# The second block's gathers and diagonals issued earlier, subtractions and casts moved between engines, in a ternary feed-forward kernel

## The chip, the cores and the metric

One core of a Trainium2 chip runs the whole kernel. The metric is the time of one execution on the device in microseconds (us). The kernel before was run three times: median 1070.45 us, from 1069.66 to 1070.65. One further execution was recorded by the hardware profiler; it took 1070.15 us, and its recorded span is 1068.3 us.

The engines are named as in the profile: PE is TensorE (matrix multiplication), PEld its weight loads, DVE is VectorE, ACT is ScalarE, POOL is GpSimd, SP is SyncE, which issues most transfers. Each engine runs its own instructions in order and waits on semaphores for the others.

## The reference

Cut to what matters, the reference computes:

```python
u  = einsum('bct,bcd->bdt', x, weights[conditions])   # x: 128 x 64 x 512, weights: 200 x 64 x 64
W1q = ternarize(W1); W2q = ternarize(W2)              # W1: 2048 x 512, W2: 512 x 2048
h  = gelu(einsum('bsd,hd->bsh', u, W1q) + b1)         # exact GELU
y  = einsum('bsh,dh->bsd', h, W2q) + b2
out = x + fake_quant_4bit(y)                          # one scale for the whole of y

def ternarize(W):
    delta = 0.05 * max|W|;  mask = |W| > delta
    alpha = sum(|W| where mask) / max(sum(mask), 1)
    return alpha * sign(W) * mask
```

Every one of the 128 samples has its own 64 x 64 matrix, chosen by `conditions`. The 128 x 64 = 8192 rows ("tokens") then pass through two ternary layers. A layer's alpha is known only when its whole weight matrix has been compared with the threshold, and the threshold only when the whole matrix has been read.

## The kernel before, in words

**Tiling.** The samples are taken in pairs, four pairs (512 tokens) to a block, 16 blocks (`NB`). In a block each pair is multiplied by a 128 x 128 block-diagonal matrix that holds two samples' matrices (`mix`, in four matmuls of 128 columns). The hidden dimension is taken in 16 chunks of 128 (`NH`). For a chunk, layer 1 (`layer1`) is eight matmuls of 512 columns: four slices of the input times two, because each activation is split into a rounded high part and the remaining low part (`split`: a copy by ScalarE, a subtraction by VectorE) so that the multiplication keeps full precision. `bend` applies GELU with alpha as its scale on ScalarE and splits the result in the same way. Layer 2 (`layer2`) is eight matmuls of 512 columns for each chunk, accumulated over the 16 chunks in four PSUM tiles `py`.

**Weights.** Signs and masks of the weights are kept as ternary values `terns` (W1) and `terns2` (W2), in four groups of four chunks. Before a chunk is multiplied, `widen1` or `widen2` casts its ternary weights to the 32-bit type of the matmul into one of four small buffers (`w1f`, `w2f`), mostly on GpSimd. From the second block on the weights are kept in 8 bits (`w1t`, `w2t`), made by `kept` on ScalarE.

**The start.** The change concerns only block 0 and the making of block 1's inputs. While W1 arrives, 54 matmuls into an unused tile (`idle`, L286 to L289) keep TensorE busy. GpSimd issues four gathers, one for each pair (`fetch`, L185: a row of `weights` for every partition, through an indirect transfer that GpSimd issues itself), into four buffers `wg`, and copies them onto the block diagonal of `diag` (`place`, L197: two copies of 64 x 64). VectorE takes the maximum of |W1|; a copy and a transpose on TensorE spread it over the partitions (`spread`, L229), in program order behind the idle matmuls; then come the threshold, block 0's mixes (`mix0`) and their splits (`hi0`, `lo0`), the masks (`mask1`), the products with the signs (`signed1`) and the first weight casts.

**Alpha of W1.** `count1` counts a group's mask by eight matmuls with a matrix of ones into `number`; `above1` sums max(|W| - delta, 0) on ScalarE. `alpha_1` (L492) reduces both: the count first, then, after its `yield`, the sums through a small matmul `total`. No GELU can run before alpha, so `early` runs layer 1 ahead into five PSUM slots, and `early_bend` follows. Chunk 5 needs the slot of chunk 0, and so its GELU. In program order the matmuls are: chunks 0 and 1, count of group 0, chunk 2, count 1, chunk 3, counts 2 and 3, total, chunk 4.

**The rest of block 0.** A loop over hc = 5 to 15 runs chunk hc of layer 1, the cast for chunk hc + 2 and `early_bend(hc - 4)`. `behind` places W2's work between: maxima (`largest2`), threshold (in `ahead` for hc = 11), and `signed2(g)`, the ternary values of W2's group g: a compare into half `g % 2` of the tile `junk` and a combined compare and subtract, both on VectorE. The low part of the split of chunks 0, 2, 4, 6, 8, 10 and 12 is a subtraction on GpSimd, at once; that of the others is put off (`open_low`) and issued on VectorE by `low`. The casts of chunks 7, 9, 11, 13 and 15 are on ScalarE. A second loop over hc = 0 to 13 (L645) runs layer 2 of block 0, the cast for chunk hc + 2, `kept`, the counts `count2(g)` on ScalarE (into half `g % 2` of `junk` again), the sums `sum2` on VectorE, and for block 1 a gather in each of hc = 0 to 3, a `place` in each of hc = 4 to 7, and a mix with its split (`condition`) in hc = 6, 8, 10 and 12. The order of instructions on each engine is the program's order (`InOrder`, L47). Layer 1 of block 1 follows; from block 2 to 12 a seven-product scheme with fewer matmuls (`seven`) takes its place, and at the end the scale of the quantization is found and all of x is read again to write the output.

Of the kernel before, what the change touches and what calls it, by code (L numbers as in the profile page):

```python
# [58 lines left out]
def tile_cond_ternary_ffn(  # L59
# [12 lines left out]
    pe, act, dve, pool, sp = (  # L72
        InOrder(tc, e) for e in (nc.tensor, nc.scalar, nc.vector, nc.gpsimd, nc.sync)
    )
    B, C, T = x.shape
    S, _, D = weights.shape
    NT = T // P
    NH = W1.shape[1]
    assert 2 * C == P and 2 * D == P and C == D and W1.shape == (P, NH, NT, P)
    PAIRS = 4  # L80
    BLK = PAIRS * P
    NB = B // (2 * PAIRS)
    NG = 4
# [51 lines left out]
    for g in range(NG):  # L135
        w = big.tile([P, GH, T], F32, tag="big", name=f"nat1_{g}")
# [6 lines left out]
    for g in range(NG):  # L143
        w = big.tile([P, GH, T], F32, tag="big", name=f"nat2_{g}")
# [30 lines left out]
    def half_of(h):  # L175
        return slice(h * C, (h + 1) * C)
# [8 lines left out]
    def fetch(n, j):  # L185

        pair = n * PAIRS + j
        wg = gather.tile([P, D], F32, tag="wg", name=f"wg_{pair}")
        pool.indirect_dma_start(
            out=wg[:, :],  # L190
            out_offset=None,
            in_=table,
            in_offset=bass.IndirectOffsetOnAxis(ap=rows[:, pair : pair + 1], axis=0),
        )
        return wg

    def place(j, wg):  # L197
        for h in range(2):
            pool.tensor_copy(diag[half_of(h), j, h * D : (h + 1) * D], wg[half_of(h), :])
# [36 lines left out]
    def thresholds(w, top, room):  # L236

        top1 = const.tile([P, 1], F32, name=f"top1_{w}")
        dve.tensor_reduce(top1, top, AX.X, ALU.max)
        delta = const.tile([P, 1], F32, name=f"delta_{w}")  # L240
        tops = spread(top1, delta, room)
        yield
        dve.tensor_reduce(delta, tops, AX.X, ALU.max)
        dve.tensor_scalar(delta, delta, THRESHOLD, None, ALU.mult)
        minus = const.tile([P, 1], F32, name=f"minus_{w}")
        dve.tensor_scalar(minus, delta, -1.0, None, ALU.mult)
        yield delta, minus
# [9 lines left out]
    def flat(w):  # L257
        return w.rearrange("p a b -> p (a b)")
# [4 lines left out]
    terns = [big.tile([P, 2, WCH], BF16, tag="big", name=f"terns_{i}") for i in range(2)]  # L263
# [5 lines left out]
    def group1(tiles, g):  # L269
        return tiles[g // 2][:, g % 2, :]  # L270

    def sign1(g):
        act.activation(group1(signs, g), flat(nat1[g]), AF.Sign)
# [11 lines left out]

    idle = ps_h.tile([P, T], F32, tag="ph", name="idle")  # L286
    pool.memset(above[:, :T], 1.0)
    for _ in range(54):
        pe.matmul(out=idle, lhsT=ones_b, rhs=above[:, :T], start=True, stop=True)  # L289
    at = 0  # L290
    for g in range(NG):
# [12 lines left out]
    fetched = [fetch(0, j) for j in range(PAIRS)]  # L304
# [13 lines left out]
    def lo0(j):  # L318
        part = slice(j * P, (j + 1) * P)
        dve.tensor_tensor(  # L320
            two_next[1][:, :, part], pcs[j], two_next[0][:, :, part], ALU.subtract
        )

    find = thresholds("w1", top_1, first[:, 3, :P])
# [7 lines left out]
    def mask1(g, part=slice(0, WCH)):  # L332

        dve.tensor_scalar(
            group1(masks, g)[:, part], flat(mags[g])[:, part], delta1, None, ALU.is_gt
        )

    def signed1(g, part=slice(0, WCH)):
        dve.tensor_tensor(
            group1(terns, g)[:, part],  # L340
            group1(masks, g)[:, part],
            group1(signs, g)[:, part],
            ALU.mult,
        )

    def count1(g, number, first, final):
        n = number.shape[1]
        for i in range(WCH // n):
            pe.matmul(
                out=number,  # L350
                lhsT=ones_b,
                rhs=group1(masks, g)[:, i * n : (i + 1) * n],
                start=(first and i == 0),
                stop=(final and i == WCH // n - 1),
            )
# [22 lines left out]
    def widen1(n, hc):  # L378

        if n == 0:  # L380
            w = w1f[hc % 4]
            g, i = divmod(hc, GH)
            src = group1(terns, g)[:, i * T : (i + 1) * T]
            if hc > 6 and hc % 2 == 1:
                act.copy(flat(w), src)
            else:
                pool.tensor_copy(flat(w), src)
        else:
            w = w1f[hc % 2]
            pool.tensor_copy(flat(w), w1t[:, hc])  # L390
        wide1[n, hc] = w
# [16 lines left out]
    def layer1(n, hc, ph, pieces=1, between=None):  # L408

        w = wide1.pop((n, hc))  # L410
        for i in range(pieces):
            part = slice(i * BLK // pieces, (i + 1) * BLK // pieces)
            for c in range(NT):
                if between is not None and c == NT // 2:
                    between()
                for k in range(2):
                    pe.matmul(
                        out=ph[:, part],
                        lhsT=w[:, c, :],
                        rhs=cond[n][k][:, c, part],  # L420
                        start=(c == 0 and k == 0),
                        stop=(c == NT - 1 and k == 1),
                    )

    def bend(n, hc, ph, two, hf, engine=dve):
        act.activation(hf, ph, AF.Gelu, bias=b1t[:, hc : hc + 1], scale=alpha[1])
        if engine is None:
            act.copy(two[0], hf)
            open_low[n, hc] = lambda: dve.tensor_tensor(two[1], hf, two[0], ALU.subtract)
        else:  # L430
            split(hf, *two, engine)
        hidden[n, hc] = two
# [3 lines left out]
    def low(n, hc):  # L436

        open_low.pop((n, hc), lambda: None)()
# [36 lines left out]
    def early(hc, between=None):  # L475

        slot = (hc + 1) % 5
        if slot < 2:
            ph = ps_h.tile([P, BLK], F32, tag="ph", name=f"ph_0_{hc}")
        else:  # L480
            ph = ps_y.tile([P, BLK], F32, tag=f"py{slot - 2}", name=f"ph_0_{hc}")
        layer1(0, hc, ph, 2 if hc == 0 else 1, between)
        waiting[hc] = ph

    def early_bend(hc):
        if hc % 2 == 0:
            pairs0[hc // 2] = big.tile([P, 2, 2, BLK], F32R, tag="big", name=f"h_{hc}")
        two = [pairs0[hc // 2][:, hc % 2, k, :] for k in range(2)]
        on_pool = hc % 2 == 0 and hc < NH - 2
        bend(0, hc, waiting.pop(hc), two, ring[hc % len(ring)], pool if on_pool else None)  # L490

    def alpha_1():  # L492
# [67 lines left out]

    mask1(0, parts1[0])
    signed1(0, parts1[0])
    widen1(0, 0)
    widen1(0, 1)
    lo0(0)
    lo0(1)
    hi0(2)
# [12 lines left out]
    number = ps_y.tile([P, T // 2], F32, tag="py3", name="number")  # L580
    count1(0, number, True, False)
    mask1(1)
    signed1(1)
    widen1(0, 4)
    mask1(2)
    mask1(3)
    early(2)
    count1(1, number, False, False)
    early(3)
    count1(2, number, False, False)  # L590
    count1(3, number, False, True)
    find = alpha_1()
    next(find)
    signed1(2)
    next(find, None)
    widen1(0, 5)
    early(4)
    early_bend(0)
# [3 lines left out]
    find = thresholds("w2", top_2, above.bitcast(F32)[:, :P])  # L602
# [6 lines left out]
    def behind(hc):  # L609
        if 5 <= hc < 5 + NG:  # L610
            largest2(hc - 5)
        if hc == 6:
            sign1(3)
        if hc == 9:
            signed1(3)
        if hc == 11:
            delta.extend(next(find))
            signed2(0)
        if hc == 12:
            low(0, 1)  # L620
            low(0, 3)
            signed2(1)
        if hc in (13, 14):
            widen2(0, hc - 13)
# [7 lines left out]
        behind(hc)  # L632
    for hc in range(NH - 4, NH):
        early_bend(hc)
    for hc in (5, 7, 9, 11):
        low(0, hc)

    w1t = big.tile([P, NH, T], F8, tag="big", name="w1t")
# [6 lines left out]
    for hc in range(NH - LAG):  # L645
        if hc + 2 < NH - LAG:
            widen2(0, hc + 2)
        layer2(0, hc)
        if hc < PAIRS:
            fetched.append(fetch(1, hc))  # L650
        elif hc < 2 * PAIRS:
            place(hc - PAIRS, fetched[hc])
        if hc == 0:
            signed2(2)
        if hc == 1:
            for i in (13, 14, 15):
                low(0, i)
        if hc < NG:
            kept(w1t, hc, terns)
        if hc == 3:  # L660
            signed2(3)
        if hc == 4:
            two_next = parts(1)
            w2t = big.tile([P, NH, T], F8, tag="big", name="w2t")
        if 4 <= hc < 4 + 2 * NG:
            g = (hc - 4) // 2
            if hc % 2 == 0:
                count2(g)
            else:
                kept(w2t, g, terns2)  # L670
        if hc in (6, 8, 10, 12):
            j = (hc - 6) // 2
            condition(1, j, pair_of(x_next, j), two_next)
            sum2(j)
    cond[1] = two_next
    x_next, two_next, fetched = [], [], []
# [282 lines left out]
    while s < len(steps):  # L959
        n, hc = steps[s]  # L960
# [116 lines left out]
```

## Time and profile before

| what | value |
|---|---|
| median of three runs | 1070.45 us (1069.66 to 1070.65) |
| profiled execution | 1070.15 us |
| its span | 1068.3 us, 16722 instructions |
| PE busy (matmul) | 990.0 us, 93% |
| DVE busy | 610.8 us, 57% |
| ACT busy | 614.4 us, 58% |
| POOL busy | 629.5 us, 59% |
| granted TensorE clock, 0 to 1000 us | 1.00 |

The parts of the profile that are used below: a table of busy times by stretch (the stretch, its length, then busy time and number of instructions of PE, PEld, DVE, ACT and POOL, then the granted clock, the DMA share and GB/s); the chain of waits, which follows the work that ended last back to the start (start, duration, what; "xN" is a number of instructions in one piece); and the timeline of one engine (start, duration, engine, line, operation, output <- inputs, shapes; in brackets the idle time before it and what ended that). Line L55 stands for nearly everything, since a helper on that line issues the instructions; so instructions are told apart by their tiles. The names are those of the program: `wg` a gather, `diag` a diagonal, `wf` a widened weight, `ph` layer 1's result, `py` layer 2's, `pc` a mix, `ring` a GELU's output, `h` its split parts, `x` the split inputs.

### The profile page before, as it was taken

To read this page: it belongs to the slowest core of one execution; us is meant where nothing else is said; L and a number is where in the kernel's file an instruction comes from. 1 tells how busy PE (TensorE), PEld (TensorE's weight loads), DVE (VectorE), ACT (ScalarE), POOL (GpSimd) and SP (SyncE) were. 2 spreads that over 40 slices of the span, in tenths; PEclk is the share of its full clock that TensorE was granted. 3 is DMA by queue.
4 is the path that set the end of the run, shared out by engine and by line. 5 is a ranking of instruction groups with operands and counts; after the bars stand their busy time and mean duration, and the time that the engine had idled before them with its cause. 6 is when DMAs were issued, how large, how long until landed. Compare 5 with 4: busy or idle time off the path is not lost.

```text
span 1068.3 us, 16722 instructions
## 1 busy us (share of the span) xinstructions
PE 990.0 (93%) x5764; PEld 864.0 (81%) x5765; DVE 610.8 (57%) x1075; ACT 614.4 (58%) x1045; POOL 629.5 (59%) x1014
## 2 busy tenths in 40 slices
PE   8989999999999999999999999999999999999400
PEld 5768889999999999999999999999998888888300
DVE  7786736565656556565656656565655223231692
ACT  7885445666666666656666665666655334334481
POOL 4595747676666667576666667576664435333242
PEclk9999999999999999999999999999999999999855
DMA  9100000100000010100000010001001010041899
GB/s 363 47 25 1 14 31 6 30 15 22 23 19 26 15 32 5 31 14 24 23 22 24 13 33 4 30 17 30 16 21 42 3 40 6 1 148 30 294 412 374
DMA packets 26611, 62.19 MB, mean 58 GB/s; under 512 B 3488, under 2 KB 3488, under 8 KB 25760
## 3 DMA queue, kind: packets, MB, share of 16 engines
q1 hardware_dynamic: 19872, 42.25, 11.7%
q0 software_dynamic: 6656, 18.88, 4.6%
q8 instruction: 46, 0.75, 0.3%
q14 instruction: 37, 0.30, 0.1%
HBM read 44.34 MB, written 16.78 MB: 57 GB/s over the span
## 4 chain that ended last, share of the span: by engine, by line
PE 91%; DMA 3%; DVE 2%; ACT 2%; POOL 1%; issue 1%; SPq 1%; POOLq 0%; DVEq 0%; ACTq 0%
PE py L55 43%; PE xy L55 16%; PE ph L55 13%; PE z L55 12%; PE pc L55 5%; DMA xt<-in_x 3%; PE idle L55 1%; DVE y L55 1%; ACT diag L55 1%; SPq L55 1%; POOL wg L55 0%; POOL diag L55 0%; ACT ring L55 0%; PE number L55 0%; DVE ymax L55 0%
## 5 line engine op out<-in xcount | busy, mean ns | idle before, releaser
L55 PE MATMUL py<-wf,h 128*128 128x512 f32 x2048 | 532.6, 395 | 4.4 <-POOL wf L55 3.5
L55 PEld LDWEIGHTS py<-wf,h 128*128 128x128 f32 x2048 | 364.9, 189 | 70.4 <-POOL wf L55 5.5
L55 DVE TENSOR_TENSOR h<-ring,h 128x512 fp32r<-128x512 f32 x249 | 193.8, 780 | 182.6 <-ACT h L55 182.6
L55 POOL CAST wf<-w2t 128x512 fp32r<-128x512 fp8e4 x242 | 173.0, 715 | 151.3 <-PE py L55 147.7
L55 ACT ACTIVATE ring<-ring,b1t,alpha_w 128x512 f32<-128x512 f32 x176 | 144.3, 820 | 97.9 <-DVE ring L55 97.9
L55 POOL CAST wf<-w1s 128x256 fp32r<-128x256 fp8e4 (+1 forms) x264 | 133.9, 512 | 110.0 <-PE xy L55 80.6
L55 POOL CAST wf<-w1t 128x256 fp32r<-128x256 fp8e4 (+1 forms) x240 | 156.9, 659 | 56.9 <-PE ph L55 45.6
L55 ACT CAST h<-ring 128x512 fp32r<-128x512 f32 x256 | 158.9, 621 | 8.2
L55 PE MATMUL ph<-x,wf 128*128 128x512 f32 (+1 forms) x648 | 158.2, 388 | 2.4 <-ACT ring L55 1.7
L55 ACT ACTIVATE ring<-ph,b1t,alpha_w 128x512 f32<-128x512 f32 x80 | 62.3, 779 | 141.9 <-PE ph L55 141.8
L55 PEld LDWEIGHTS ph<-x,wf 128*128 128x128 f32 x648 | 119.8, 188 | 28.7 <-issue 2.4
L55 DVE TENSOR_TENSOR ring<-xy,ring 128x256 f32<-128x256 f32 (+1 forms) x176 | 97.2, 552 | 64.3 <-PE xy L55 64.3
L55 PEld LDWEIGHTS xy<-xt,wf 128*128 128x128 f32 x704 | 107.6, 189 | 14.1
L55 PE MATMUL xy<-xb,wf 128*128 128x256 f32 x704 | 112.4, 281 | 0.0
L55 PE MATMUL xy<-xt,wf 128*128 128x256 f32 x704 | 111.8, 282 | 0.0
L55 PEld LDWEIGHTS xy<-xb,wf 128*128 128x128 f32 x704 | 102.2, 190 | 7.9
L55 ACT COPY ring<-xy 128x256 f32<-128x256 f32 x176 | 65.1, 370 | 67.8 <-PE xy L55 67.7
L55 PE MATMUL z<-xt,wf 128*128 128x256 f32 x704 | 98.3, 282 | 0.0
L55 ACT COPY ring<-z 128x512 f32<-128x512 f32 x88 | 51.7, 588 | 73.9 <-DVE h L55 73.3
L55 PEld LDWEIGHTS z<-xt,wf 128*128 128x128 f32 x704 | 90.2, 190 | 0.0
L55 DVE TENSOR_TENSOR xt<-x_quarters,xt 128x512 fp32r<-128x512 f32 x44 | 33.8, 768 | 90.9 <-ACT xt L55 90.9
L55 POOL DMA_INDIRECT wg<-in_L_cond_weights,rows x64 | 76.3, 1193 | 11.4 <-issue 5.4
(104 smaller groups left out, 857.7 us busy)
## 6 DMA issues: line engine op xcount, KB each, us to landing
xt<-in_x SPq DMA_DIRECT2D x36, 512.0 KB, 6.6
out<-y POOLq DMA_DIRECT2D x30, 512.0 KB, 12.5
x_quarters<-in_x SPq DMA_DIRECT2D x48, 256.0 KB, 2.6
nat<-in_L_ffn_W SPq DMA_DIRECT2D x6, 1024.0 KB, 10.1
nat<-in_L_ffn_W SPq DMA_DIRECT2D x3, 512.0 KB, 9.0
wg<-in_L_cond_weights,rows POOLq DMA_INDIRECT x64, 2.7
w1t<-in_x SPq DMA_DIRECT2D x4, 256.0 KB, 2.7
w2t<-in_x SPq DMA_DIRECT2D x4, 256.0 KB, 2.6
```

Of the source, the lines that this page charges most:

```text
L55: return lambda *args, **kw: self._tc.keep_in_program_order(make(*args, **kw))
```

## The change

Six edits, all ahead of the second block's layer 1:

- 50 idle matmuls in place of 54.
- The casts of chunks 7, 9, 11, 13 and 15 of W1 go from ScalarE to GpSimd.
- GpSimd keeps the subtractions of chunks 0, 2, 4 and 6; those of 8, 10 and 12 are put off and done by VectorE (`low`), in a new grouping: 5, 7, 8, 9 behind layer 1, and 10 to 15 in the second turn of layer 2's loop.
- Block 1's gathers move out of layer 2's loop: three ahead of the first two weight casts on GpSimd, the fourth behind them. Its diagonals are placed behind the cast of chunk 4, ahead of that of chunk 5.
- Layer 1 of chunk 3 comes behind all counts; `signed1(2)` ahead of the count's reduction; the total of alpha's sums is issued within chunk 3, ahead of its last slice.
- `sign1(3)` moves one chunk back, and block 1's mixes one turn forward, to hc = 5, 7, 9 and 11.

```diff
-    for _ in range(54):
+    for _ in range(50):
         pe.matmul(out=idle, lhsT=ones_b, rhs=above[:, :T], start=True, stop=True)
...
-            src = group1(terns, g)[:, i * T : (i + 1) * T]
-            if hc > 6 and hc % 2 == 1:
-                act.copy(flat(w), src)
-            else:
-                pool.tensor_copy(flat(w), src)
+            pool.tensor_copy(flat(w), group1(terns, g)[:, i * T : (i + 1) * T])
...
-                if between is not None and c == NT // 2:
+                if between is not None and c == NT - 1:
                     between()
...
-        on_pool = hc % 2 == 0 and hc < NH - 2
+        on_pool = hc in (0, 2, 4, 6)
...
     signed1(0, parts1[0])
+    fetched += [fetch(1, j) for j in range(3)]
     widen1(0, 0)
     widen1(0, 1)
+    fetched += [fetch(1, 3)]
     lo0(0)
...
     widen1(0, 4)
+    for j in range(PAIRS):
+        place(j, fetched[PAIRS + j])
     mask1(2)
     mask1(3)
+    signed1(2)
     early(2)
-    count1(1, number, False, False)
-    early(3)
-    count1(2, number, False, False)
-    count1(3, number, False, True)
+    for g in range(1, NG):
+        count1(g, number, False, g == NG - 1)
     find = alpha_1()
     next(find)
-    signed1(2)
-    next(find, None)
+    early(3, lambda: next(find, None))
     widen1(0, 5)
     early(4)
     early_bend(0)
...
-        if hc == 6:
+        if hc == 7:
             sign1(3)
...
-    for hc in (5, 7, 9, 11):
+    for hc in (5, 7, 8, 9):
         low(0, hc)
...
-        if hc < PAIRS:
-            fetched.append(fetch(1, hc))
-        elif hc < 2 * PAIRS:
-            place(hc - PAIRS, fetched[hc])
...
         if hc == 1:
-            for i in (13, 14, 15):
+            for i in range(10, NH):
                 low(0, i)
...
-        if hc in (6, 8, 10, 12):
-            j = (hc - 6) // 2
+        if hc in (5, 7, 9, 11):
+            j = (hc - 5) // 2
             condition(1, j, pair_of(x_next, j), two_next)
```

More of the change, by code (lines that the diff above doesn't have):

```diff
@@ L619, in behind @@
         if hc == 12:
-            low(0, 1)
-            low(0, 3)
+            for i in (1, 3):
+                low(0, i)
             signed2(1)
```

## The prediction

> **What bounds the kernel now.** I read the page first (one core, span 1068.3 us, the profiled execution 1070.15 us, so 1.85 us lie around the span; the median of the runs shown is 0.30 us above that execution). Then the busy time by stages:
>
> ```profile
> 20.00:40.00 20.00, 17.98 (x106) 14.24 (x105) 16.55 (x19) 16.21 (x19) 9.79 (x10) 1.00 0.36 146
> 40.00:60.00 20.00, 19.63 (x88) 15.83 (x87) 17.14 (x14) 19.62 (x30) 14.21 (x11) 1.00 0.19 54
> 60.00:80.00 20.00, 15.02 (x65) 10.76 (x64) 17.32 (x14) 15.20 (x13) 18.90 (x21) 1.00 0.10 34
> 80.00:100.00 20.00, 20.00 (x103) 17.02 (x102) 11.40 (x12) 12.49 (x14) 11.98 (x12) 1.00 0.00 0
> 180.00:1000.00 820.00, 819.13 (x4919) 729.42 (x4918) 441.40 (x876) 462.66 (x862) 493.04 (x835) 1.00 0.09 27
> ```
>
> After the stretch come TensorE (matmuls, then loads), VectorE, ScalarE, GpSimd. From 80 us to 1000 us TensorE is full, so the change, which lies wholly ahead of that, is worth exactly what it takes from the start of the second block's layer 1. In the chain of waits that start is the "PE ph" piece at 93.28:
>
> ```profile
> 16.23 1.03 PE idle L55 x4
> 17.26 0.11 PE tops_delta_w L55
> 34.96 0.79 ACT ring L55
> 57.66 3.64 PE py L55 x16
> 67.56 2.83 POOL wg L55
> 71.18 0.64 POOL wg L55
> 74.28 2.35 POOL diag L55
> 91.45 1.83 PE py L55 x8
> 93.28 1.81 PE ph L55 x8
> ```
>
> Three places lose time: the warm-up still runs when the threshold could be spread (VectorE's copy ends at 15.84 + 0.23 = 16.07); alpha (34.87) holds the first GELU and so layer 1 of chunk 5 (35.88); and from 61 to 77 us layer 2's weight casts queue on GpSimd behind subtractions, gathers and diagonals. The last takes 93.28 - 57.66 = 35.62 us for 14 layer-2 chunks (1.82 each, 25.5) and four mixes (0.89 each, 3.56): 6.6 us lost.
>
> The timeline of ScalarE shows a second limit:
>
> ```profile
> 60.68 7.30 ACT L55 CAST w1t<-terns 128x2048 fp8e4<-128x2048 bf16 x4
> 69.58 1.91 ACT L55 ACTIVATE junk<-terns 128x2048 bf16<-128x2048 bf16 x1 [1.60 <-DVE terns L55]
> 76.55 1.91 ACT L55 ACTIVATE junk<-terns 128x2048 bf16<-128x2048 bf16 x1 [3.17 <-DVE terns L55]
> ```
>
> The count of group 1 overwrites the junk half that signed2(3) uses, so it waits for signed2(3)'s end at 76.51. Behind it on ScalarE stand the casts that split the second block's inputs.
>
> [...] four GpSimd casts at 23.74 took 1.6 us apiece, ending in step with VectorE's masks and products, where alone they take 0.59. [...] gathers took 0.94 us early and 1.23 to 2.83 here. [...] here idle matmuls reach 0.213 us from 8.03 on, so four fewer at the end leave the clock warm.
>
> **The change part by part.**
>
> *Four fewer idle matmuls.* 41 took 8.73 us, so 4 x 0.213 = 0.85. The spread could then start at 16.25, after 16.07: -0.85 on the threshold, mixes and masks.
>
> *Gathers early.* Three gathers go ahead of the first weight casts on GpSimd, which idles from 15.93 to 19.60. The early row gives 1.48 + 1.28 + 1.26 us with gaps, to 19.95; the mask and product run meanwhile (17.1 to 18.6), so I take 20.2. First cast to 20.8 (before 20.19), so layer 1 starts at about 20.9 and its second half at about 21.8, against 22.34: 0.5 of the 0.85 survives. Bounds: [...] each gather at the 2.83 row plus 0.17 gap ends at 24.9, which makes that start 4.8 later than 20.70. The fourth gather (1.3 to 2 us) fits before widen1(0,2), whose input is ready at about 22.8. Their transfers (6.2 us to landing under the weight load) are back by 29 us, in time for the diagonals. SP's queue is not passed.
>
> *Diagonals early.* Eight copies of 0.23 us stand between widen1(0,4) and widen1(0,5). VectorE then runs two masks and signed1(2); one small copy slips between two of these, so three are done by 30 and five more by 31.6, then widen1(0,5) by 32.2. It is needed at 34. On VectorE I charge 0.3 us more for these interruptions (bounds 0 and 1.5, the excess of 0.35 per cast seen on the masks times four).
>
> *Counts ahead of chunk 3, alpha within it.* Masks end near 29.0, the last count near 30, signed1(2) is now ahead of the count's reduction (1.21) and hidden, since ScalarE's sums end at 31.74 - 0.85 = 30.9 anyway. TensorE meanwhile does three quarters of chunk 3 (1.4), then the total (0.12). Alpha is at about 32, not 34.87. TensorE has the rest of chunk 3 and chunk 4 to about 34.1; the GELU ends at 32.9. So chunk 5 starts at 34.1, not 35.88: -1.8 (bounds -2.3 and 0).
>
> *ScalarE's five casts to GpSimd, GpSimd's three subtractions to VectorE.* ScalarE loses 5 x 0.62 = 3.1 us, so one chunk takes 1.33 there against 1.82 on TensorE; even with sign1(3) (1.81) behind chunk 3, chunk 9 has 1 us to spare. GpSimd gains 5 x 0.61 and loses subtractions of 3.29, 1.74 and 3.31. Layer 1 then runs 11 x 1.822 + 0.11 = 20.15 without the former stalls (1.6): it ends at 54.25, not 57.66. Moving sign1(3) one chunk back costs nothing: signed1(3) waits for VectorE's four reductions (8.86) longer. Layer 2 and mixes, 29.06 us, would end at 83.3.
>
> *VectorE's chain to signed2(3).* It starts when the second threshold's transpose runs ahead of chunk 11: 34.1 + 6 x 1.82 + 0.3 + 0.7 = 46.1, say 46.2 (before 49.29). It holds 4 x (1.28 + 2.35) = 14.5 and now twelve subtractions, not nine: 12 x 0.69 = 8.3; 22.8 in all. Before, the same minimum was 20.7 and the measured length 27.2[...]. I estimate about 14 casts there now, some 8 us of work, giving 4.5 (4.1 by ratio, 4.9 at 0.35 each). So 27.3, and signed2(3) ends at 73.5, not 76.51.
>
> *ScalarE after it.* Count 1.91 + kept 1.80 + split cast 0.56, then rounds of 4.18 (80.72 to 84.90): the last split cast ends 12.7 after signed2(3), VectorE's low part 13.4 after. Layer 1 of the second block starts at 73.5 + 13.45 = 86.95. TensorE stands some 3.6 us here: this is the new wait, "PE ph from DVE x".
>
> **Sum.** 93.28 - 86.95 = 6.3 us gained. The profiled 1070.15 becomes 1063.85 (span 1062.0), the median 1070.45 becomes **1064.1**. Nothing behind the point changes order, and the tail (39 us of transfers) starts that much earlier.
>
> **Rivals.**
>
> *TensorE alone bounds (12 in 100).* [...] its chain has the minimum: 45.7 + 22.8 = 68.5, plus 13.45 = 82. TensorE then sets 82.8 and the gain is 10.5: 1060.0. For: GpSimd is relieved of all gathers. Against: its casts are there, and each one contends.
>
> *The early gathers hold the first cast (13 in 100 for it and lesser delays).* At 3.0 us each layer 1 starts at 25.5; 12.9 us of work follow, chunk 5 starts at 38.4, the second chain at about 50.5, signed2(3) at 77.8, the second block at 91.2: 1068.4, the edge of no change. Milder forms end between 1066.5 and 1068. [...]
>
> *Same (8 in 100).* Two half-measures of this kind together, within 0.2%: 1068.3 to 1072.6, which is about what a measurement can tell from no change.
>
> *Slower (7 in 100).* [...] At the worst means and longest seen (2.32 + 2.86 per group, 1.40 per subtraction) its chain is 4 x 5.18 + 12 x 1.40 = 37.5; signed2(3) ends at 83.7 and the second block starts at 97.1, 3.9 later: 1074.3. It turns slower where signed2(3) passes 79.8, a chain over 33.6. For: VectorE is the busiest feeder in that stretch. Against: GpSimd's long subtractions, its worst partner, leave it.
>
> The likeliest (60 in 100) lies between gains of 4 and 9: 1061.5 to 1066.5. The range for 8 in 10 is 1060.2 to 1068.0. Faster 0.85, same 0.08, slower 0.07.
>
> **What would show it.** The spread at 16.25; gathers on GpSimd from 15.95 and the first cast ending near 20.8; GELU 0 near 32, chunk 5 at 34.1 with no wait on the ring; layer 2 starting near 54.3 and no wait on casts in it; signed2(3) ending near 73.5, ScalarE's second count waiting for it; a TensorE idle of about 3.6 us ahead of the second block's layer 1 at 87. Wrong, if that idle is absent (then faster), or if the first cast or signed2(3) comes as late as before.

## The result, and the profile after

The changed kernel takes 1063.66 us in the median (1062.84 to 1064.56), the kernel before, run beside it, 1070.5. The ratio is 0.9938, 95% interval 0.9921 to 0.9955: faster by 0.45% to 0.79%. The forecast was 1064.1. The profiled execution took 1062.89 us, its span is 1061.0 us.

The busy times of the changed kernel by the same stretches (columns as before: TensorE, its loads, VectorE, ScalarE, GpSimd, then the granted clock):

```profile
20.00:40.00 20.00, 19.43 (x111) 16.06 (x110) 18.69 (x18) 18.42 (x20) 16.50 (x22) 1.00 0.39 154
40.00:60.00 20.00, 20.00 (x90) 16.51 (x89) 17.84 (x18) 19.46 (x27) 18.09 (x14) 1.00 0.27 80
60.00:80.00 20.00, 20.00 (x106) 17.15 (x105) 18.20 (x16) 14.62 (x13) 9.66 (x9) 1.00 0.00 1
80.00:100.00 20.00, 17.73 (x74) 13.17 (x74) 13.39 (x21) 9.55 (x13) 9.68 (x12) 1.00 0.01 2
```

TensorE is now full from 40 to 80 us, where it was at 19.63 and 15.02 of 20; but from 80 to 100, where it was full, 2.3 us are missing. So the wait moved. The chain of waits says to where. Pieces of it, in order:

```profile
15.76 0.25 POOL diag L55
18.97 0.95 POOL wg L55
20.63 4.01 PE ph L55 x24
31.54 13.39 PE ph L55 x58
44.92 0.12 PE tops_delta_w L55
63.41 4.85 DVE h L55 x6
69.85 2.61 DVE terns L55
72.49 2.00 ACT junk L55 x2
84.63 0.50 ACT x L55
85.15 0.70 DVE x L55
85.89 1.89 PE ph L55 x7
```

Before, between 20 us and the second block, this chain ran mainly on TensorE, ScalarE and GpSimd's gathers and diagonals. Now it leaves TensorE at the transpose of W2's threshold (44.92), runs through VectorE to the end of signed2(3) at 72.46, through ScalarE's counts, `kept` casts and split casts to 85.13, and comes back at 85.89, where "PE ph" is layer 1 of the second block. That is 7.39 us earlier than the 93.28 of before, and the spans differ by 7.3.

The wait itself, in ScalarE's and TensorE's timelines of the changed kernel (in brackets the idle time and what ended it):

```profile
72.49 1.91 ACT L55 ACTIVATE junk<-terns 128x2048 bf16<-128x2048 bf16 x1 [4.77 <-DVE terns L55]
```

```profile
85.26 0.47 PE L55 MATMUL ph<-x,wf 128*128 128x512 f32 x1 [2.10 <-ACT x L55]
85.89 1.89 PE L55 MATMUL ph<-x,wf 128*128 128x512 f32 x7 [0.16 <-DVE x L55]
```

ScalarE stands 4.77 us for signed2(3) before its second count, and TensorE 2.26 us for the split behind it.

### The profile page after: what moved, and what is told of

It reads as the page before. It is cut to its first block, busy times and chain, and to the rows that moved or that the text cites. A ratio compares the mean times of both kernels' runs of the same rounds, so it can differ in the third digit from the quotient of the medians.

```text
span 1061.0 us, 16715 instructions
## 1 busy us (share of the span) xinstructions
PE 986.1 (93%) x5760; PEld 864.0 (81%) x5761; DVE 610.9 (58%) x1078; ACT 611.4 (58%) x1040; POOL 628.2 (59%) x1016
## 4 chain that ended last, share of the span: by engine, by line
PE 87%; DVE 4%; DMA 3%; ACT 2%; issue 1%; POOL 1%; SPq 1%; POOLq 0%; DVEq 0%; ACTq 0%
PE py L55 42%; PE xy L55 16%; PE ph L55 13%; PE z L55 12%; PE pc L55 5%; DMA xt<-in_x 3%; DVE h L55 1%; DVE y L55 1%; ACT diag L55 1%; DVE terns L55 1%; POOL wg L55 1%; ACT junk L55 1%; SPq L55 1%; DVE junk L55 1%; DMA wg<-in_L_cond_weights,rows 1%
## 5 line engine op out<-in xcount | busy, mean ns | idle before, releaser
L55 DVE TENSOR_TENSOR xt<-x_quarters,xt 128x512 fp32r<-128x512 f32 x44 | 33.8, 768 | 91.1 <-ACT xt L55 91.1
L55 POOL DMA_INDIRECT wg<-in_L_cond_weights,rows x64 | 73.5, 1148 | 11.7 <-issue 4.4
```

The costliest lines, as they stand in the source:

```text
L55: return lambda *args, **kw: self._tc.keep_in_program_order(make(*args, **kw))
```

## The experiments

All times are medians; each kernel was run beside the kernel before, whose medians in these sets were 1070.16 to 1070.47. The changed kernel was in none of these sets, so a comparison with its 1063.66 goes across sets. The changed kernel's own executions spread over 1.7 us, so differences under about 1 us from 1063.66 are not read as effects.

### Gathers and diagonals back in layer 2's loop

```diff
-    fetched += [fetch(1, j) for j in range(3)]
...
-    fetched += [fetch(1, 3)]
...
-    for j in range(PAIRS):
-        place(j, fetched[PAIRS + j])
...
+        if hc < PAIRS:
+            fetched.append(fetch(1, hc))
+        elif hc < 2 * PAIRS:
+            place(hc - PAIRS, fetched[hc])
```

> The changed kernel with the second block's gathers and diagonals back in layer 2's loop (gathers in hc 0 to 3, diagonals in hc 4 to 7), all else as changed. Theory (the chain VectorE signed2(3) -> ScalarE's counts and split casts sets the second block, TensorE has 2.3 us to spare ahead of it): GpSimd's gathers fit between casts[...]; signed2(3) ends 1 to 2 us later than 72.5, and the time rises by 1 to 2 us, to some 1065. Rival (the gathers were the gain, 5 to 6.6 us of it): casts of layer 2 stall TensorE as before, and the time rises by 4 to 6 us, to some 1068.

Measured: 1063.19 us. Nothing is lost. TensorE does wait for a diagonal again (its timeline):

```profile
66.51 1.16 PE L55 MATMUL pc<-diag,xt 128*128 128x128 f32 x8 [1.90 <-POOL diag L55]
85.92 1.88 PE L55 MATMUL ph<-x,wf 128*128 128x512 f32 x7 [0.16 <-DVE x L55]
```

The 1.90 us come out of the 2.1 it would have stood later; layer 1 of the second block starts at the same 85.9. The rival is out. So is the first theory's 1 to 2 us: signed2(3) ends at 72.47 here. VectorE's chain (from its first compare to the end of signed2(3)) takes 27.1 us instead of 26.7. But four gathers and five of the copies took the place of three casts on GpSimd in that time (12 instead of 15), so the 0.4 us is not what gathers and copies cost it by themselves.

### Three subtractions back on GpSimd

```diff
-        on_pool = hc in (0, 2, 4, 6)
+        on_pool = hc % 2 == 0 and hc < NH - 2
```

> The changed kernel with the subtractions of chunks 8, 10 and 12 back on GpSimd. Theory: VectorE's chain has three subtractions less (2.1 to 2.4 us)[...]; signed2(3) ends within 1 us of 72.5 and the time stays within 1 us of the changed kernel. Rival (moving the subtractions off GpSimd was needed): layer 2's casts come late behind them, TensorE stalls at chunk 0 or 1 of layer 2 by 1.5 to 3 us, and the time rises by 2 us or more.

Measured: 1063.62 us. The chain from the first compare to signed2(3)'s end is 27.4 us (45.67 to 73.1) against 26.7, with nine subtractions on VectorE instead of twelve; the author had reckoned that GpSimd's three would bring back about 2 us of the 2.1 to 2.4 that VectorE saves (an estimate). The casts come late, as the rival has it, and TensorE waits 1.89 and 0.57 us for them at chunks 1 and 2 of layer 2, but again out of its slack: in this profile the second block starts at 86.54, 0.65 us later, still behind VectorE's split.

### The counts of W2 in one half of the junk tile

```diff
-            junk[:, g % 2, :], group2(g), AF.Square,
+            junk[:, 0, :], group2(g), AF.Square,
```

> The changed kernel with one edit: all counts of W2 write their unused output to half 0 of the junk tile, so that the count of group 1 no longer waits for signed2(3). Theory: ScalarE's second count then starts right behind the split cast at 67.7, the last split cast ends near 80, VectorE's last low part near 82, and TensorE's own work (83.1) sets the second block: 2.3 to 2.8 us less, some 1061.2. Rival (VectorE's own chain, with sum2 and the low parts behind signed2(3), sets it): the low part of the last mix stays near 85.9, and the time is unchanged.

Measured: 1059.8 us, ratio to the kernel before 0.9907 (0.989 to 0.9923). ScalarE's second count and TensorE, from their timelines in this run:

```profile
67.44 1.91 ACT L55 ACTIVATE junk<-terns 128x2048 bf16<-128x2048 bf16 x1
```

```profile
79.09 3.89 PE L55 MATMUL py<-wf,h 128*128 128x512 f32 x16
82.81 1.98 PE L55 MATMUL ph<-x,wf 128*128 128x512 f32 x8
```

The count starts 5 us earlier without a wait, and layer 1 of the second block follows layer 2 without a gap: 82.98 in the chain of waits, 2.9 us before the changed kernel. The last low part on VectorE ends at 81.77, so the rival, VectorE's own tail, is not the limit. This is the bound of the changed kernel, shown by taking away what made the wait.

### The gathers alone, on the kernel before

```diff
+    fetched += [fetch(1, j) for j in range(3)]
     widen1(0, 0)
     widen1(0, 1)
+    fetched += [fetch(1, 3)]
...
     widen1(0, 4)
+    for j in range(PAIRS):
+        place(j, fetched[PAIRS + j])
...
-        if hc < PAIRS:
-            fetched.append(fetch(1, hc))
-        elif hc < 2 * PAIRS:
-            place(hc - PAIRS, fetched[hc])
```

> The kernel before with one part of the change alone: gathers ahead of and behind the first two casts, diagonals behind the cast of chunk 4. Theory: most of the 6.6 us that layer 2 of block 0 loses to GpSimd goes; what is left is the wait of its third cast behind the subtraction of chunk 12 (about 1.6 us)[...]; second block at about 88.3, not 93.3: 5 us less, some 1065.5. Rival (the gain is alpha's): within 1 us of the kernel before.

Measured: 1068.74 us, ratio 0.9986 (0.9979 to 0.9993): 1.5 us gained, not 5. TensorE did get its casts in time, all but one:

```profile
62.75 9.36 PE L55 MATMUL py<-wf,h 128*128 128x512 f32 x40 [1.65 <-POOL wf L55]
86.36 2.07 PE L55 MATMUL py<-wf,h 128*128 128x512 f32 x8
89.72 0.47 PE L55 MATMUL ph<-x,wf 128*128 128x512 f32 x1 [1.29 <-ACT x L55]
90.88 1.89 PE L55 MATMUL ph<-x,wf 128*128 128x512 f32 x7 [0.69 <-DVE x L55]
```

Its own work ends at 88.3, as expected, but layer 1 waits until 90.88 for the split. signed2(3) ends at 76.43 here, 0.1 us from the kernel before and not about 2 us earlier, as the author had estimated: with the gathers gone and casts in their place, VectorE's chain takes 27.3 us (49.10 to 76.43), against 27.2.

### The same, with the counts in one half

> The kernel before with the early gathers and diagonals (as in the run of that part alone) and all counts of W2 into half 0 of the junk tile. Theory: what the early gathers free on TensorE was taken back by ScalarE's wait for signed2(3); with that wait gone the second block starts at about 88.3 instead of 90.9, and the time is some 2.6 us below the early gathers alone, 1066.1. Rival (something else holds the mixes' splits): no change from 1068.7.

The edits of the last two runs together, on the kernel before. Measured: 1065.87 us, and layer 1 of the second block at 88.14:

```profile
86.22 2.07 PE L55 MATMUL py<-wf,h 128*128 128x512 f32 x8
88.14 1.98 PE L55 MATMUL ph<-x,wf 128*128 128x512 f32 x8
```

The gathers alone had fallen 3.2 us short of what was expected; 2.9 of it lay in ScalarE's wait for signed2(3), which the kernel before hid behind TensorE's waits for casts.

### Counts, chunk 3 and alpha as before

```diff
-    signed1(2)
     early(2)
-    for g in range(1, NG):
-        count1(g, number, False, g == NG - 1)
+    count1(1, number, False, False)
+    early(3)
+    count1(2, number, False, False)
+    count1(3, number, False, True)
     find = alpha_1()
     next(find)
-    early(3, lambda: next(find, None))
+    signed1(2)
+    next(find, None)
```

> The changed kernel with the counts, chunk 3, signed1(2) and alpha in the order of before. Theory (the gain comes through the start of VectorE's chain, and so through alpha and chunk 5): alpha at about 34.1 instead of 32.0, chunk 5 at 35.0 instead of 33.8, signed2(3) 1.2 later, time 1.2 us more than the changed kernel, some 1064.8. Rival (TensorE has slack ahead of the second block, so alpha's place is worth nothing): within 0.3 us of it.

Measured: 1065.91 us, 2.2 us more than the changed kernel. TensorE's timeline:

```profile
35.57 2.08 PE L55 MATMUL ph<-x,wf 128*128 128x512 f32 x8 [1.28 <-ACT ring L55]
38.07 9.41 PE L55 MATMUL ph<-x,wf 128*128 128x512 f32 x40 [0.41 <-POOL wf L55]
```

The two waits that the kernel before has there are back: for the GELU of chunk 0, and for the cast of chunk 6, which stands behind chunk 0's subtraction on GpSimd and so behind alpha too. The first compare of VectorE's chain starts at 48.33 instead of 45.78, signed2(3) ends at 75.0, and the second block starts at 88.45. Some 0.3 us of that is not alpha's: in this execution the idle matmuls end at 16.48 instead of 15.13, as where the clock first wakes late, and layer 1 begins at 20.95 instead of 20.63. Of the parts taken back alone this one cost the most, but its 2.2 us and the 1.8 us of the mixes' order, further down, are not told apart within the spread.

### Four more idle matmuls

```diff
-    for _ in range(50):
+    for _ in range(54):
```

> The changed kernel with 54 idle matmuls. Theory: where the clock wakes late (12 slow matmuls) they end at 17.0 and the threshold is 0.9 later; where it wakes early (7 slow) they end at 16.0 and nothing changes; since the gathers now set the first cast, at most 0.75 of it reaches chunk 0's second half. So 0 to 0.75 us more, some 1064.0. Rival (the warm-up is still what starts the chain): 0.9 us more in every run.

Measured: 1064.98 us (1063.4 to 1065.95), 1.3 more than the changed kernel, with both spreads over 1.7 us: a cost, but its size is not settled. The profiled execution was one of the lower ones (1063.4); its transpose starts at 16.10 as with 50, and the second block at 86.22, 0.33 later. So that 0.33 does not come from a later end of the idle matmuls, and no trace of a slower execution was taken.

### ScalarE's five casts back

```diff
-            pool.tensor_copy(flat(w), group1(terns, g)[:, i * T : (i + 1) * T])
+            src = group1(terns, g)[:, i * T : (i + 1) * T]
+            if hc > 6 and hc % 2 == 1:
+                act.copy(flat(w), src)
+            else:
+                pool.tensor_copy(flat(w), src)
```

> The changed kernel with the casts of chunks 7, 9, 11, 13 and 15 back on ScalarE. Theory: ScalarE then needs 1.64 us a chunk on the mean, against 1.82 on TensorE, and with sign1(3) the ring is late by 0.2 to 0.4 us at chunks 9 and 10; time 0.4 us more. Rival (these casts were what stalled layer 1 before, 1.6 us in all): 1.3 to 1.6 us more, some 1065.2.

Measured: 1062.54 us, 1.1 us less than the changed kernel. Layer 1's 58 matmuls take 13.76 us instead of 13.53, as the theory has it; but VectorE's chain, begun at 46.43, ends at 72.33: 25.9 us instead of 26.7. VectorE's subtractions at its start lost their partners:

```profile
50.33 1.70 DVE L55 TENSOR_TENSOR h<-ring,h 128x512 fp32r<-128x512 f32 x2
```

In the changed kernel the same two take 2.11. Only 13 casts on GpSimd overlap the chain, instead of 15. How much is gained is less sure: the changed kernel's executions lie in two pairs (below, in the last section), and against the lower one, 1062.84 and 1062.89, it is 0.3 us. Either way that part of the change is worth nothing in the changed kernel.

### Each cast of W2 made twice

```diff
-            pool.tensor_copy(w, group1(terns2, g)[:, i * T : (i + 1) * T])
+            for _ in range(2):
+                pool.tensor_copy(w, group1(terns2, g)[:, i * T : (i + 1) * T])
```

> The changed kernel with each of block 0's 14 casts of W2 on GpSimd made twice (same output). Theory (GpSimd instructions[...] hold up VectorE's chain by about 0.35 us each): some 12 more lie in the chain, signed2(3) ends near 76.5 instead of 72.5, and the time rises by 3 to 4 us, to some 1067. Rival (the chain's length is VectorE's own work[...]): signed2(3) within 1 us of 72.5, time within 1 us of the changed kernel.

Measured: 1066.19 us. The chain is 28.7 us long (45.75 to 74.4), 2.0 more, not 4. For example, the six subtractions that took 4.93 us in the changed kernel take 6.18 (VectorE's timelines, the changed kernel first):

```profile
63.33 4.93 DVE L55 TENSOR_TENSOR h<-ring,h 128x512 fp32r<-128x512 f32 x6
```

```profile
64.06 6.18 DVE L55 TENSOR_TENSOR h<-ring,h 128x512 fp32r<-128x512 f32 x6
```

How many casts met the chain is counted over its length in both kernels (busy time and number for TensorE, its loads and GpSimd, of the instructions on `wf` alone; the changed kernel first):

```profile
45.78:72.46 26.68, 25.39 (x111) 20.43 (x110) 19.94 (x15) 1.00 0.10 32
```

```profile
45.75:74.41 28.66, 25.46 (x101) 19.38 (x99) 28.09 (x21) 0.94 0.09 29
```

Not 12 but six more casts lie in the chain, 21 instead of 15, since GpSimd ran casts without a break from 45.40 to 82.46 and got no further. That is 0.33 us for each, about the price put on them; it was their number that was wrong. The time is not a clean measure of it: TensorE waited for the doubled casts itself, up to 2.06 us in one place, and set the second block at 89.1. Half of that delay is another effect, the clock:

```profile
64.67 5.50 PE L55 MATMUL py<-wf,h 128*128 128x512 f32 x16 [2.06 <-POOL wf L55]
```

Sixteen such matmuls take 3.89 us elsewhere; behind this gap the granted clock was 0.50 for 3.41 us.

### Block 1's mixes one turn later, as before

```diff
-        if hc in (5, 7, 9, 11):
-            j = (hc - 5) // 2
+        if hc in (6, 8, 10, 12):
+            j = (hc - 6) // 2
```

> The changed kernel with block 1's mixes in turns 6, 8, 10 and 12 of layer 2's loop, as before. Theory: the second block is set by ScalarE and VectorE behind signed2(3), and in this order the first split cast stands behind the second count and the last low part behind the third sum; it starts 14.4 after signed2(3), as in the run of the early gathers alone, not 13.4: 1.0 us more, some 1064.6. Rival (TensorE's order does not matter there): unchanged.

Measured: 1065.49 us (1063.96 to 1066.7). signed2(3) ends at 72.4 and the second block starts about 14.5 later, as expected (13.4 in the changed kernel). The profiled execution took 1066.08, and its table of stretches shows why it lost more than the 1.0 us:

```profile
84.14:87.55 3.41, 1.19 (x4) 0.82 (x5) 3.41 (x4) 1.39 (x2) 2.39 (x3) 1.00 0.00 0
87.55:90.97 3.42, 3.42 (x10) 2.65 (x9) 1.79 (x2) 1.26 (x2) 2.82 (x2) 0.50 0.00 0
```

The column behind the five engines is the granted clock: TensorE was busy for only 1.19 of 3.41 us, and the clock stood at 0.50 for the next 3.41. Seven matmuls of layer 1 took 2.76 us there (1.89 in the changed kernel) and eight of layer 2 took 2.74 (1.99): 1.6 us. With the 0.94 us by which the second block starts later this makes 2.5 of the 3.2 us between the two profiled executions; the rest arises behind the last block.

### A shorter start

The counts in one half, 44 idle matmuls, and two gathers on each side of the first casts:

```diff
-    for _ in range(50):
+    for _ in range(44):
...
-    fetched += [fetch(1, j) for j in range(3)]
+    fetched += [fetch(1, j) for j in range(2)]
     widen1(0, 0)
     widen1(0, 1)
-    fetched += [fetch(1, 3)]
+    fetched += [fetch(1, j) for j in range(2, 4)]
...
-            junk[:, g % 2, :], group2(g), AF.Square,
+            junk[:, 0, :], group2(g), AF.Square,
```

> The changed kernel with the counts of W2 in one half, 44 idle matmuls and two of the gathers ahead of the first casts, two behind. Theory: with ScalarE's wait gone TensorE is full from the first cast on; the first cast comes at about 19.2 instead of 20.6, TensorE starts layer 1 behind its mixes at 20.1 instead of 20.5, and the threshold no longer depends on when the clock wakes: 0.3 to 0.8 us below the run with the counts in one half alone, some 1059.3, with less spread. Rival (fewer idle matmuls let the clock fall back, or the start has another bound): the same or slower than 1059.8.

Measured: 1060.37 us (1059.37 to 1062.23). The rival was right. TensorE's timeline and the stretches of this run:

```profile
16.16 0.48 PE L55 MATMUL tops_delta_w<-ident_f,first 128*128 128x128 f32 x1 [2.09 <-DVE first L55]
16.43 5.24 PE L55 MATMUL pc<-diag,xt 128*128 128x128 f32 x32
```

```profile
12.75:16.16 3.41, 1.32 (x8) 0.40 (x5) 3.28 (x6) 3.38 (x3) 1.63 (x7) 1.00 1.06 381
16.16:19.57 3.41, 3.41 (x16) 3.41 (x17) 2.53 (x6) 2.47 (x2) 3.02 (x4) 0.50 1.05 420
```

TensorE stands 2.1 us without work ahead of the transpose, and the clock is at 0.50 for the next 3.41; the 32 matmuls of the mixes take 5.24 us, where the changed kernel has 3.75. The profiled execution is the slowest of the four (1062.23); what the other three did is not seen.

### The same with 50 idle matmuls

> The changed kernel with the counts of W2 in one half and two of the gathers ahead of the first casts, two behind, with its 50 idle matmuls. Theory (in the run with 44 idle matmuls the clock fell back in the 2 us without work ahead of the threshold's transpose, and hid what the earlier cast gives): the clock stays at 1.00 through the mixes, layer 1 starts behind the mixes at 20.1, some 0.3 us below the counts in one half alone, 1059.5, with none of the executions above 1061. Rival (the division of the gathers itself costs time at the start): 1060.4 or more, as with 44.

Measured: 1059.12 us (1059.07 to 1059.6), ratio to the kernel before 0.9896 (0.988 to 0.9913). Layer 1's first matmuls follow the mixes at once:

```profile
16.27 3.74 PE L55 MATMUL pc<-diag,xt 128*128 128x128 f32 x32
19.76 1.32 PE L55 MATMUL ph<-x,wf 128*128 128x256 f32 x9
```

So the division of the gathers is harmless, and the idle matmuls made the difference. This version has the lowest median of all that were run, about 4.5 us below the changed kernel.

## Why the prediction was right

The likeliest case came true, by its mechanism and nearly by its numbers. That the median agrees to 0.4 us is in part luck: it lies between two pairs of executions, at about 1062.9 and 1064.5, where no execution lies. The profiled execution, forecast at 1063.85, took 1062.89; the 1.0 us is a chain on VectorE that starts 0.4 earlier and is 0.6 shorter than forecast.

| step | forecast | profile after |
|---|---|---|
| threshold's transpose | 16.25 | 16.15 |
| first cast ends | 20.8 | 20.6 |
| alpha | about 32 | 32.04 |
| chunk 5 of layer 1 | 34.1 | about 33.8 (31.54 + 10 of 58 matmuls in 13.39) |
| first compare of VectorE's chain | 46.2 | 45.78 |
| length of that chain | 27.3 | 26.7 |
| signed2(3) ends | 73.5 | 72.46 |
| from there to the second block | 13.45 | 13.43 |
| second block's layer 1 | 86.95 | 85.89 |
| TensorE idle ahead of it | 3.6 | 2.26 |

*What bounds the kernel after* was the step that carried it. The wait of the second count had to be read from a bracket in a stretch where it cost nothing (3.17 us, while TensorE waited for casts), and followed over ScalarE's order to the mixes' splits. The run with the counts in one half shows it. (The forecast start of VectorE's chain adds up to 46.0, not 46.1; nothing hangs on it.)

*The part by part prices* were partly right for other reasons. Alpha's order was put at 1.8 us together with the threshold; taken back alone it costs 2.2, since the cast of chunk 6 waits for alpha too.

*The 4.5 us that VectorE's chain was to lose to GpSimd* were an estimate: before, the chain took 6.5 us more than its minimum (27.2 against 20.7), and the author set these against some 12.3 us of GpSimd's work. That gave nearly the right length, but in part by luck, since one ratio for all of GpSimd's work does not hold. The price of 0.35 us for a cast does: six more casts in the chain made it 2.0 us longer (0.33 each), two fewer 0.8 shorter (0.4 each). At 0.33 to 0.4 a cast, the four gathers and five copies of the run with the gathers back, where the chain is 0.4 us longer with three casts fewer, cost it some 1.4 to 1.6 us, an estimate; that is little for the 13 us that they took on GpSimd there. The three subtractions cost the most: back on GpSimd they make the chain 0.7 us longer, though VectorE then does 2.1 us less and meets one cast less, so some 3 us by the same estimate. The change takes out gathers, copies and subtractions, and lets seven more casts in (15 against 8) and 2.1 us more of VectorE's own work: the chain is 26.7 us long, against 27.2. By what means GpSimd's work makes VectorE's longer, no run shows; these lengths are what was measured.

*"ScalarE loses 3.1 us"* and the stalls of 1.6 us that were to go with the casts: the profile shows no stall after, but the run with these casts back on ScalarE shows none of 1.6 us either. Once alpha is early, the ring has room for both.

*Four fewer idle matmuls*, priced at a flat 0.85 us: the price depends on when the clock wakes. In the kernel before 12 idle matmuls ran slowly, until 8.03 us; in the profile after only 7, until 5.9, so TensorE even stood 1.03 us ahead of the transpose. What four more cost in the changed kernel is not settled (1.3 us in the median).

*The rival of the gathers* that hold the first cast came about only in small: they took 0.98, 1.11 and 0.95 us in the 4 us ahead of it. But the chain of waits after does run through them, and with the gathers back in layer 2's loop layer 1 starts at 19.66 instead of 20.63; its first two chunks then end 0.4 us earlier (24.25 instead of 24.64). As for the gain as a whole, it is not a sum of parts. Taken back one at a time, gathers, subtractions and casts each cost nothing in the median, and the waits on TensorE that come back with the first two are swallowed by its slack of about 2 us; taken alone, the gathers give 1.5. The order of alpha, which starts the chain that now bounds, can't be taken back free. Two of the GpSimd parts taken back together were not tried.

## What to carry to other kernels

A wait that costs nothing today, because its engine is not the bound, is the first candidate for the bound after the change: follow it forward before putting down the gain. Look whether an unused output makes it; here one index in a scratch tile was worth about 3 us in the profiles (3.9 in the medians). And a part whose removal changes nothing in the finished kernel may only be covered by the slack that another wait leaves.

## What the runs showed of the hardware

The prediction did not reckon with a fall of the clock. It is seen in three traces, at a cost of 1.5 to 1.6 us each: behind gaps of 2.1 us (44 idle matmuls), 2.06 us (casts doubled) and about 3 us with one matmul inside (mixes as before). Gaps of 1.03 and 2.1 us in the changed kernel's profile left it at 1.00, so the length of a gap alone does not decide.

What does is seen when a trace is cut into stretches of 3.41 us, counted from the moment at which its clock first woke. Each of the three falls lasted one such stretch and began on a boundary, 3, 17 and 24 stretches after the waking. Stretches with little work for TensorE, from the runs with doubled casts and with the gathers back, and from the changed kernel:

```profile
61.26:64.67 3.41, 1.35 (x7) 0.76 (x5) 3.38 (x3) 2.04 (x2) 3.35 (x3) 1.00 0.00 0
64.67:68.08 3.41, 3.41 (x8) 2.73 (x9) 3.41 (x4) 3.30 (x3) 3.28 (x4) 0.50 0.00 0
```

```profile
64.68:68.09 3.41, 1.58 (x11) 1.49 (x12) 3.41 (x5) 3.23 (x4) 3.03 (x5) 1.00 0.03 10
68.09:71.50 3.41, 3.41 (x18) 2.84 (x17) 3.38 (x3) 0.21 (x1) 3.29 (x4) 1.00 0.02 5
```

```profile
80.97:84.38 3.41, 2.19 (x10) 1.49 (x8) 2.90 (x3) 3.41 (x3) 0.00 (x0) 1.00 0.00 0
84.38:87.80 3.42, 2.38 (x9) 1.78 (x10) 2.65 (x2) 0.74 (x2) 3.05 (x3) 1.00 0.00 0
```

TensorE was busy for 1.19, 1.32 and 1.35 us in the stretches ahead of the three falls (35 to 40%). In all other stretches of the 14 traces, up to 989 us, it was busy for 1.58 us (46%) or more (the lowest is 1.91 in the kernel before and 2.19 in the changed one), and none is followed by a fall. At the end, where the matmuls run out, each of the 14 clocks falls right behind the first stretch with 35% or less (9% in the kernel before, whose clock falls at 1004.71 us; 33% in the changed one, at 995.74). In the changed kernel a boundary cuts the gap ahead of the second block in two, which leaves 64% and 70%. So 35 to 40% of work in a stretch did not prevent a fall. Where between 40 and 46% the bound lies, and whether busy time is what counts, no run shows.

The moment at which the clock first wakes differs between executions whose first 5 us are the same: after 6, 7, 9 or 12 slow idle matmuls in the traces here. So the boundaries, counted from there, lie elsewhere in each execution, and a gap of the same length can cost 1.6 us or nothing. The executions of the changed kernel lie in two pairs, 1062.8 to 1062.9 and 1064.4 to 1064.6. A stretch that took in the whole of its gap of 2.26 us would have some 1.15 us of work (an estimate, 34%), and a fall there would fit the 1.6 between the pairs; no trace of the higher pair was taken, so this is argued only. The spreads fit too: kernels with a gap of about 2.3 us or more there spread over 1.7 to 2.7 us (the changed kernel, alpha as before, 54 idle matmuls, mixes as before); without it, counts in one half and the same with 50 idle matmuls spread over 0.9 and 0.5.
